# Two attention layers on one core: projections in half blocks, and four split steps in the second layer

## The chip, the core and the metric

The kernel runs on one core of a Trainium2 chip. The core has five engines with queues of their own, which wait for each other through semaphores: PE (TensorE, matrix products; its weight loads are shown as PEld), DVE (VectorE, elementwise work), ACT (ScalarE, exponentials and copies), POOL (GpSimd) and SP (SyncE, which here only issues DMAs). The metric is the device time of one execution, in microseconds (us).

## What is computed

Two self-attention layers over four images of 64 x 64 pixels (4096 tokens) with 256 channels, in float32. Cut to what matters:

```python
# layer 0: queries and keys have 32 channels, values 256
q, k, v = x @ Wq + bq, x @ Wk + bk, x @ Wv + bv
x = gamma * softmax(q @ k.T) @ v + x
# layer 1: queries and keys have 32 channels, values 128, then back to 256
f, g, v = x @ Wf + bf, x @ Wg + bg, x @ Wh + bh
x = x + (softmax(g @ f.T) @ v) @ Wo + bo
```

The softmax runs over all 4096 tokens of an image, and the result is x after both layers.

## The kernel before

**Stages.** Image after image, first layer, then second layer. The code calls the layers `l = 0` and `l = 1`. A block of queries is 256 tokens in the first layer (16 blocks) and 512 in the second (8 blocks). Each block runs over all keys in steps: 8 steps of 512 keys in the first layer, 16 steps of 256 keys in the second. So every step has 128 x 1024 scores, and there are 128 steps per layer and image, 1024 in all. The list `steps` (line 645) holds them, and the loop of line 654 walks it.

**A step.** `Step.scores` (line 498) multiplies keys by queries into the PSUM tile `st`, of which there is only one, and ACT takes the exponential into `p`. The scores of step s are issued two steps ahead (`later`, line 685). [...] So some steps are *split*: ACT writes a second exponential `high`, a little smaller than `p` (line 515); DVE forms `low = p - high` (line 522, one step ahead) and `d` from low and high (line 527); the values are cut in the same way into h, l and d; and three F32R products (high, low, d) take the place of one plain product (`products_first`, line 531, `products_second`, line 544). In the first layer all steps are split. In the second those with `i % 5 == 2`: steps 2, 7 and 12 of each block (line 248). In the second layer DVE also adds every `p` to `p_sum` (line 698), since the softmax's divisor comes from there; line 696 opens it with a copy at each block's first step.

**Projections.** `project_units` (line 405) makes queries, keys and values of one block of 512 tokens, as a list of units: a transpose unit (line 371: DVE turns 32 x 32 squares that eight DMAs of `load_squares`, line 267, have laid out; ACT and DVE cut the result into two parts xh and xl), a qk unit (line 408: four matmuls of 512 columns into `psqk`, four small operations on ACT and DVE, a store to `qk_dram`, from which POOL's queue later loads `k` and `q`), and one or two value units (line 437). The queries, keys and values of the second layer are projected while the first layer still runs over later blocks, and those of the next image's first layer during the second layer. Values of the second layer live in the tags `v1` (plain) and `v1_parts` (split). For image 0, `AHEAD = 3` blocks are projected before the first step and the others in the steps of the first block (`early`, line 689), through PE transposes of `x_nat`.

**Ends.** `end_first` (line 566) normalises a block of the first layer, adds the residual and stores the result as x1_dram (for the projection) and x1_res (for the second residual). `end_second` (line 607) gives four output units, each two matmul groups (`pso`), a reciprocal, a multiply-add and a store.

**Order.** Units wait in a list `units`: the end units of the block before, then projections. Lines 702 to 705 release them at an even pace per step. The engines' queues may depart a little from the order in the program, for instance where the profile shows six products between two scores.[...]

Of the kernel before, what the change touches and what calls it, by code (L numbers as in the profile page):

```python
# [55 lines left out]
P = 128  # L57
QB = 512
# [4 lines left out]
EPS = 2.0**-12  # L63
AHEAD = 3

# [168 lines left out]
def fast_path(ctx: ExitStack, tc: tile.TileContext, x, w0, w1, wo, bo, gamma, out, off):  # L234
# [13 lines left out]
    split = [[l == 0 or i % 5 == 2 for i in range(NI[l])] for l in range(2)]  # L248
# [18 lines left out]
    def load_squares(key, tokens):  # L267

        turned[key] = []
        for c in range(NCC):  # L270
            t = work.tile([P, QB], F32, tag="squares", bufs=5, name=f"squares_{key[0]}_{key[1]}_{key[2]}_{c}")
            for a in range(P // S):
                ch = c * P + a * S
                nc.sync.dma_start(
                    t[a * S : (a + 1) * S, :].rearrange("j (b i) -> j b i", i=S),
                    tokens[:, ch : ch + S].rearrange("(b j) i -> j b i", j=S),
                )
            turned[key].append(t)

    def load_block(b, j):  # L280
        if b < B and j < NB:
            load_squares((b, 0, j), x[b, j * QB : (j + 1) * QB, :])


    x_nat = {}

    def load_first(j):
        if j < NB:
            x_nat[j] = []
            for n in range(j * NT, (j + 1) * NT):  # L290
                x_nat[j].append(data.tile([P, C], F32, tag="v1", bufs=V1, name=f"x_nat_{n}"))
                nc.sync.dma_start(x_nat[j][-1], x[0, n * P : (n + 1) * P, :])

    load_first(0)
    load_first(1)
# [8 lines left out]
    seen_v = const.tile([P, 2, B * NB, 2], F32, name="seen_v")  # L304
# [61 lines left out]
    xT, x_parts, k_t, v_t = {}, {}, {}, {}  # L366
# [4 lines left out]
    def transpose_unit(b, l, j):  # L371
        def issue():
            xT[b, l, j] = data.tile([P, NCC, QB], F32, tag="xT", name=f"xT_{b}_{l}_{j}")
            for c in range(NCC):
                if b == l == 0:
                    ps = side_psum(f"psx_{j}_{c}")
                    for t in range(NT):
                        nc.tensor.transpose(ps[:, t * P : (t + 1) * P], x_nat[j][t][:, c * P : (c + 1) * P], ident)
                    nc.scalar.copy(xT[b, l, j][:, c, :], ps)
                else:  # L380
                    nc.vector.transpose(xT[b, l, j][:, c, :], turned[b, l, j][c])
            x_parts[b, l, j] = []
            for c in range(NCC):
                parts = [
                    work.tile([P, QB], F32R, tag="squares", bufs=5, name=f"x{what}_{b}_{l}_{j}_{c}") for what in "hl"
                ]
                nc.scalar.copy(parts[0], xT[b, l, j][:, c, :])  # L387
                nc.vector.tensor_sub(parts[1], xT[b, l, j][:, c, :], parts[0].bitcast(F32))  # L388
                x_parts[b, l, j].append(parts)
            if b == l == 0:  # L390
                load_first(j + 2)
            elif l == 0:
                load_block(b, j + 1)
            elif j == NB - 1:
                load_block(b + 1, 0)

        return issue

    def split_values(v, h, low, d, seen):
        nc.scalar.activation(h, v, AF.Copy, scale=1.0 - DOWN)  # L400
        nc.scalar.activation(low, v, AF.Abs, accum_out=seen)
        nc.vector.scalar_tensor_tensor(d, h.bitcast(F32), -1.0 - EPS, v, ALU.mult, ALU.add)
        nc.vector.scalar_tensor_tensor(low, d.bitcast(F32), 1.0 / EPS, h.bitcast(F32), ALU.mult, ALU.add)

    def project_units(b, l, j):
        key = (b, l, j)

        def qk_unit():
            ps = side_psum(f"psqk_{b}_{l}_{j}")
            for c in range(NCC):  # L410
                for n in range(2):
                    nc.tensor.matmul(  # L412
                        ps,
                        wqk[l][:, c, :],
                        x_parts[key][c][n],
                        start=(c == n == 0),
                        stop=(c == NCC - 1 and n == 1),
                    )
            whole = data.tile([2 * D, QB], F32, tag="qk", name=f"qk_{b}_{l}_{j}")
            parts = data.tile([P, QB], F32R, tag="qk_parts", name=f"qk_parts_{b}_{l}_{j}")  # L420
# [6 lines left out]
            qk_dram[key] = dram.tile([2, 2, D, QB], F32, name=f"qk_dram_{b}_{l}_{j}")  # L427
            nc.sync.dma_start(qk_dram[key].rearrange("h w d n -> (h w d) n"), parts.bitcast(F32))
            if b == l == 0:
                near = parts.rearrange("(h w d) n -> h w d n", h=2, w=2)  # L430
                load_k(b, l, j, near)
                if j == 0:
                    load_q(b, l, j, near)

        per = QB // CV[l]

        def v_unit(t0):
            def issue():
                ps = side_psum(f"psv_{b}_{l}_{j}_{t0}").rearrange("p (t c) -> p t c", c=CV[l])
                for t in range(per):  # L440
                    for c in range(NCC):
                        nc.tensor.matmul(  # L442
                            ps[:, t, :],
                            xT[key][:, c, (t0 + t) * P : (t0 + t + 1) * P],
                            wv[l][:, c, :],
                            start=(c == 0),
                            stop=(c == NCC - 1),
                        )
                tiles = slice(t0, t0 + per)
                seen = [seen_v[:, l, b * NB + j, n : n + 1] for n in range(2)]  # L450
                if l == 0:
                    split_values(ps, *(v0[j][what][:, tiles, :C] for what in ("h", "l", "d")), seen[t0 // per])
                    return
                for n in range(NT // G[1]):
                    i = j * NT // G[1] + n
                    v = ps[:, n * G[1] : (n + 1) * G[1], :]
                    if split[1][i]:
                        t = data.tile([P, 3, G[1], P], F32R, tag="v1_parts", bufs=sum(split[1]), name=f"v_{b}_{i}")
                        v_t[b, i] = {what: t[:, m] for m, what in enumerate(("h", "l", "d"))}
                        split_values(v, *v_t[b, i].values(), seen[n])  # L460
                    else:
                        v_t[b, i] = data.tile([P, G[1], P], F32, tag="v1", bufs=V1, name=f"v_{b}_{i}")
                        nc.scalar.copy(v_t[b, i], v)
                        nc.scalar.activation(v, v, AF.Abs, accum_out=seen[n])  # L464

            return issue

        return [transpose_unit(b, l, j), qk_unit] + [v_unit(t0) for t0 in range(0, NT, per)]

    def load_rows(dst, parts, which, halves):  # L470
        for n, h in enumerate(halves):
            nc.gpsimd.dma_start(dst[n * D : (n + 1) * D, :], parts[h, which])  # L472

    def load_q(b, l, j, parts=None):
        q_t[b, l, j] = data.tile([P, QB], F32R, tag="q", bufs=2, name=f"q_{b}_{l}_{j}")
        load_rows(q_t[b, l, j], qk_dram[b, l, j].bitcast(F32R) if parts is None else parts, 0, (0, 0, 1, 1))

    def load_k(b, l, j, parts=None):
        k_t[b, l, j] = data.tile([P, QB], F32R, tag="k", bufs=NB, name=f"k_{b}_{l}_{j}")
        load_rows(k_t[b, l, j], qk_dram[b, l, j].bitcast(F32R) if parts is None else parts, 1, (0, 1, 0, 1))  # L480
# [8 lines left out]
    class Step:  # L489
# [28 lines left out]

# [5 lines left out]
        def cut_both(self):  # L524
            if self.split:
                self.d = wide("d" if self.l == 0 else "l", f"d_{self.key}", F32R)
                nc.vector.scalar_tensor_tensor(  # L527
                    self.d, self.low.bitcast(F32), -1.0 / EPS, self.high.bitcast(F32), ALU.mult, ALU.add
                )

# [13 lines left out]
        def products_second(self, acc):  # L544
            v = v_t[self.b, self.i]
            some = [i for i in range(NI[1]) if split[1][i]]
            for p, v, which, first, last in (
                (
                    (self.high, v["h"], 0, self.i == some[0], False),
                    (self.low, v["l"], 0, False, self.i == some[-1]),  # L550
                    (self.d, v["d"], 1, self.first, self.last),
                )
                if self.split
                else ((self.p, v, 1, self.first, self.last),)
            ):
                for g in range(G[1]):
                    nc.tensor.matmul(  # L557
                        acc[which],
                        v[:, g, :],
# [6 lines left out]
    def end_first(b, j, acc):  # L566
# [11 lines left out]
        def residual(s):  # L578
            def issue():
# [11 lines left out]
                if part == QB // QB0 - 1 and s == NS - 1:  # L591
                    load_squares((b, 1, jj), x1_dram[b, jj])
# [49 lines left out]
    for j in range(AHEAD):  # L642
        run(project_units(0, 0, j))
# [7 lines left out]
    units, done, acc, p_sum = bias_units(), 0, None, None  # L651
    keys = [(b, l, j) for b in range(B) for l in range(2) for j in range(NB)][NB:]

    for n, s in enumerate(steps):
        b, l, j = s.b, s.l, s.j
        if s.first:
            done = 0
# [139 lines left out]
```

## Time and profile before

Three runs took 3223.26, 3223.30 and 3223.58 us. The profiled execution is one further run.

| | |
|---|---|
| median of 3 runs | 3223.3 us |
| profiled execution, its own time | 3222.18 us |
| its span, first to last instruction | 3220.4 us |
| granted TensorE clock, mean | 0.998 |
| DMA, mean over the span | 53 GB/s |
| queue of SP, share of 16 engines | 16.0% |
| queue of POOL, share of 16 engines | 4.5% |

The starts of the second layer's blocks can be read from line 696, the copy that opens p_sum. The distances between them, in us:

| image | block 0 to 1 | 1 to 2 | 2 to 3 | 3 to 4 | 4 to 5 | 5 to 6 | 6 to 7 |
|---|---|---|---|---|---|---|---|
| 0 | 48.56 | 39.50 | 41.75 | 41.77 | 41.72 | 41.75 | 41.76 |
| 1 | 50.19 | 39.49 | 41.75 | 41.77 | 41.73 | 41.76 | 41.77 |
| 2 | 50.20 | 39.50 | 41.77 | 41.75 | 41.76 | 41.76 | 41.74 |
| 3 | 41.25 | 35.88 | 37.16 | 37.18 | 37.16 | 37.52 | 36.81 |

In images 0 to 2 the next image is projected beside these blocks; in image 3 there is none. In the first layer two blocks together, one with a projection and one without, take 56.5 us. The first block of the first image ends at 95 us.

The profile names an instruction by line, engine and operation, output and inputs, and the shape (partitions x elements). "x4" is a number of instructions that follow each other; a bracket at a line's end says how long the engine was idle before it and what ended the wait.

### The profile page before, as it was taken

Reading aid. Unit: us, or ns where it says so; the run is one execution under the profiler, and the core shown is the slowest. Engines: PE = TensorE matmul, PEld = TensorE weight load, DVE = VectorE, ACT = ScalarE, POOL = GpSimd, SP = SyncE. Lnnn points to the kernel's source line nnn. Section 1 sums busy time; section 2 is a strip of 40 time slices with the busy share of each in tenths; the row PEclk is TensorE's granted clock in tenths of the full one; section 3 lists DMA queues with packets and bytes.
Section 4 is the critical chain, followed back from the end, with each engine's and each line's share of the span. In section 5 each row is a group of like instructions: output and inputs, shape, how many; then the busy total and the mean of one; then the engine's idle time right before and its main releaser. Section 6 shows DMA issues by size and latency. Waiting matters only on the chain. (4 is left out here: it accounts for less than half of the span.)

```text
span 3220.4 us, 51144 instructions
## 1 busy us (share of the span) xinstructions
PE 3166.5 (98%) x19460; PEld 2613.0 (81%) x19460; DVE 2691.5 (84%) x3181; ACT 1988.8 (62%) x2483; POOL 661.3 (21%) x784
## 2 busy tenths in 40 slices
PE   8999999999999999999999999999999999999998
PEld 7999997566799999655679999966558999995554
DVE  7888888888888888788888888878888888887776
ACT  6666666655566666565556666655555666665554
POOL 3222223000232222200022222310002222241000
PEclk9999999999999999999999999999999999999999
DMA  4111123221212112322121112232222211121110
GB/s 120 47 47 44 50 50 83 56 53 49 59 44 54 44 52 49 79 53 53 49 64 42 49 50 50 61 70 52 51 52 57 53 41 47 46 70 47 36 36 31
DMA packets 368653, 172.16 MB, mean 53 GB/s; under 512 B 257392, under 2 KB 343664, under 8 KB 368400
## 3 DMA queue, kind: packets, MB, share of 16 engines
q1 hardware_dynamic: 342528, 134.29, 16.0%
q0 software_dynamic: 24960, 34.18, 4.5%
q8 instruction: 157, 2.57, 0.3%
q14 instruction: 96, 0.79, 0.1%
q10 hardware_dynamic: 912, 0.33, 0.0%
HBM read 99.22 MB, written 67.11 MB: 52 GB/s over the span
## 5 line engine op out<-in xcount | busy, mean ns | idle before, releaser
L517 ACT ACTIVATE p<-st 128x1024 f32<-128x1024 f32 x1024 | 1044.5, 1020 | 393.6 <-PE st L505 369.5
L515 ACT ACTIVATE high<-st,down 128x1024 fp32r<-128x1024 f32 x608 | 678.8, 1116 | 683.6 <-PE st L505 572.7
L527 DVE SCALAR_TENSOR_TENSOR d<-low,high 128x1024 fp32r<-128x1024 f32 x608 | 761.2, 1252 | 208.3 <-PE acc L536 202.9
L522 DVE TENSOR_TENSOR low<-p,high 128x1024 fp32r<-128x1024 f32 x608 | 810.6, 1333 | 134.2 <-ACT p L517 134.2
L557 PE MATMUL acc<-p,v 128*128 128x512 f32 x1664 | 795.2, 597 | 0.0
L505 PE MATMUL st<-q,k 128*128 128x256 f32 (+1 forms) x3072 | 778.6, 361 | 8.4 <-ACT p L517 8.3
L698 DVE TENSOR_TENSOR p_sum<-p_sum,p 128x1024 f32<-128x1024 f32 x480 | 587.1, 1223 | 60.7 <-ACT p L517 47.5
L505 PEld LDWEIGHTS st<-q,k 128*128 128x128 f32 x3072 | 461.2, 189 | 210.7 <-ACT p L517 113.3
L536 PE MATMUL acc<-v0d,d 128*128 128x258 f32 x4096 | 591.7, 284 | 1.7 <-DVE d L527 1.6
L536 PE MATMUL acc<-v0h,high 128*128 128x258 f32 x4096 | 588.6, 283 | 1.6 <-ACT high L515 1.6
L536 PE MATMUL acc<-v0l,low 128*128 128x258 f32 x4096 | 587.0, 283 | 0.5 <-DVE low L522 0.5
L536 PEld LDWEIGHTS acc<-v0d,d 128*128 128x128 f32 x4096 | 533.1, 189 | 6.7 <-DVE d L527 3.6
L536 PEld LDWEIGHTS acc<-v0h,high 128*128 128x128 f32 x4096 | 534.1, 190 | 3.4 <-ACT high L515 2.0
L536 PEld LDWEIGHTS acc<-v0l,low 128*128 128x128 f32 x4096 | 532.7, 189 | 0.8 <-DVE low L522 0.7
L557 PEld LDWEIGHTS acc<-p,v 128*128 128x128 f32 x1664 | 308.4, 190 | 214.3 <-issue 184.7
L593 POOL TENSOR_TENSOR x_res<-x,bo 128x256 f32<-128x256 f32 x128 | 216.3, 1690 | 889.9 <-DVE g L583 482.0
L472 POOL DMA_DIRECT2D q<-qk_dram x252 | 123.9, 501 | 1166.1 <-PE st L505 1143.0
L676 POOL TENSOR_TENSOR x_res<-x_res,bv 128x256 f32<-128x256 f32 x128 | 189.6, 1482 | 114.4 <-DMA x_res<-in_x 85.0
L442 PE MATMUL psv<-wv,xT 128*128 128x128 f32 (+1 forms) x1024 | 194.8, 331 | 6.8 <-DVE qk L423 6.1
L442 PEld LDWEIGHTS psv<-wv,xT 128*128 128x128 f32 x1024 | 159.6, 192 | 29.8 <-DVE qk L423 8.5
L472 POOL DMA_DIRECT2D k<-qk_dram x224 | 109.6, 500 | 245.2 <-PE st L505 140.3
L388 DVE TENSOR_TENSOR xl<-xT,xh 128x512 fp32r<-128x512 f32 x128 | 87.1, 683 | 5.1 <-ACT xh L387 4.7
(96 smaller groups left out, 1701.9 us busy)
## 6 DMA issues: line engine op xcount, KB each, us to landing
x_res<-in_x SPq DMA_DIRECT2D x128, 128.0 KB, 2.2
qk_dram<-qk_parts SPq DMA_DIRECT2D x64, 256.0 KB, 2.1
x_dram<-x SPq DMA_DIRECT2D x128, 128.0 KB, 1.7
x_res<-x_res SPq DMA_DIRECT2D x128, 128.0 KB, 1.7
squares<-x_dram SPq DMA_DIRECT2D x256, 64.0 KB, 2.3
x_old<-x_res SPq DMA_DIRECT2D x128, 128.0 KB, 2.0
out<-x_old SPq DMA_DIRECT2D x128, 128.0 KB, 1.7
q<-qk_dram POOLq DMA_DIRECT2D x252, 64.0 KB, 2.1
```

The lines of the kernel that those rows point to most:

```text
L442: nc.tensor.matmul(ps[:, t, :], xT[key][:, c, (t0 + t) * P : (t0 + t + 1) * P], wv[l][:, c, :], start=(c == 0), stop=(c == NCC - 1),)
L472: nc.gpsimd.dma_start(dst[n * D : (n + 1) * D, :], parts[h, which])
L505: nc.tensor.matmul(st[:, g, :], k_t[b, l, kt // NT][:, kt % NT * P : (kt % NT + 1) * P], q_t[b, l, j * n // QB][:, q0 : q0 + n], start=Tru ...
L515: nc.scalar.activation(self.high, s_flat, AF.Exp, bias=down)
L517: nc.scalar.activation(self.p, s_flat, AF.Exp)
L522: nc.vector.tensor_sub(self.low, self.p, self.high.bitcast(F32))
L527: nc.vector.scalar_tensor_tensor(self.d, self.low.bitcast(F32), -1.0 / EPS, self.high.bitcast(F32), ALU.mult, ALU.add)
L536: nc.tensor.matmul(acc[2 * s + which][:, :W], p[:, g * QB0 + s * P : g * QB0 + (s + 1) * P], v0[self.i][v][:, g, :], start=self.first and ...
L557: nc.tensor.matmul(acc[which], v[:, g, :], p[:, g * QB : (g + 1) * QB], start=first and g == 0, stop=last and g == G[1] - 1,)
L593: nc.gpsimd.tensor_add(x_old[s], x_new[s], bo_sb)
L676: nc.gpsimd.tensor_add(x_res[b, j][t], x_res[b, j][t], bv)
L698: nc.vector.tensor_add(p_sum, p_sum, s.p)
```

## The change

Projections are cut into halves of 256 tokens (`h`, 16 per image and layer; `QB0 = 256`, `NH = N // QB0`). A half has one transpose unit over both halves of the channels, one qk unit with four matmuls of 256 columns, and one value unit. Squares, xT, xh and xl have one buffer each. In image 0's first layer xT, xh, xl and the parts of qk use the four buffers of `v1_parts` instead. The list with a pace is replaced by `plan`, which gives each unit a step. In the second layer steps 2, 6, 10 and 14 are split instead of 2, 7 and 12.

```diff
+UP = 2.0**12
+SPLIT1 = (2, 6, 10, 14)
...
-    split = [[l == 0 or i % 5 == 2 for i in range(NI[l])] for l in range(2)]
+    NH = N // QB0
+    split = [[l == 0 or i in SPLIT1 for i in range(NI[l])] for l in range(2)]
...
     def load_squares(key, tokens):
+        t = work.tile([P, NCC, QB0], F32, tag="squares", bufs=1, name="squares_" + "_".join(map(str, key)))
         for c in range(NCC):
-            t = work.tile([P, QB], F32, tag="squares", bufs=5, name=f"squares_{key[0]}_{key[1]}_{key[2]}_{c}")
...
-    load_first(0)
-    load_first(1)
+    for h in range(LEAD):
+        load_first(h)
...
-    def transpose_unit(b, l, j):
+    def transpose_unit(b, l, h):
         def issue():
+            key = (b, l, h)
+            lead = b == l == 0
+            tag = "v1_parts" if lead else "xT"
+            xT[key] = data.tile([P, NCC, QB0], F32, tag=tag, bufs=LEAD_BUFS if lead else 1, name=f"xT_{b}_{l}_{h}")
             if b == l == 0:
+                ps = side_psum(f"psx_{h}").rearrange("p (c n) -> p c n", c=NCC)
+                for c in range(NCC):
+                    for t in range(NS):
+                        nc.tensor.transpose(ps[:, c, t * P : (t + 1) * P], x_nat[h][t][:, c * P : (c + 1) * P], ident)
+                nc.scalar.copy(xT[key], ps)
+            else:
+                nc.vector.transpose(
+                    xT[key].rearrange("p c n -> p (c n)"), turned[key].rearrange("p c n -> p (c n)")
+                )
...
+            nc.scalar.copy(x_parts[key][0], xT[key])
+            nc.vector.tensor_sub(x_parts[key][1], xT[key], x_parts[key][0].bitcast(F32))
+            if b == l == 0:
+                load_first(h + LEAD)
             elif l == 0:
-                load_block(b, j + 1)
-            elif j == NB - 1:
-                load_block(b + 1, 0)
+                load_half(b, h + 1)
+            elif h == NH - 1:
+                load_half(b + 1, 0)
...
         def qk_unit():
-            ps = side_psum(f"psqk_{b}_{l}_{j}")
+            ps = side_psum(f"psqk_{b}_{l}_{h}")[:, :QB0]
...
+            nc.sync.dma_start(qk_dram[b, l, j].rearrange("h w d n -> (h w d) n")[:, cols], parts.bitcast(F32))
+            halves[b, l, j] = part + 1
             if b == l == 0:
                 near = parts.rearrange("(h w d) n -> h w d n", h=2, w=2)
-                load_k(b, l, j, near)
+                load_k(b, l, j, cols, near)
...
-                if part == QB // QB0 - 1 and s == NS - 1:
-                    load_squares((b, 1, jj), x1_dram[b, jj])
+                if s == NS - 1:
+                    load_squares((b, 1, j), x1_dram[b, jj][part * QB0 : (part + 1) * QB0, :])
...
-    for j in range(AHEAD):
-        run(project_units(0, 0, j))
+    lead = [project_units(0, 0, h) for h in range(2 * AHEAD)]
+    run([u[0] for u in lead[:2]])
+    for h in range(2 * AHEAD):
+        run(lead[h][1:])
+        run([u[0] for u in lead[h + 2 : h + 3]])
...
+    def plan(b, l, j, ends):
+
+        units = {}
+
+        def put(i, *some):
+            units.setdefault(i, []).extend(some)
+
+        if l == 0:
+
+            if j >= 2:
+                t, qk, v = project_units(b, 1, j - 2)
+                put(0, t), put(4, qk), put(5, v)
+            for n, u in enumerate(ends):
+                put(1 + n, u)
+            return units
+        if j == 0:
+            for n, u in enumerate(ends):
+                put(1 + n, u)
+            for n, h in enumerate((NH - 2, NH - 1)):
+                t, qk, v = project_units(b, 1, h)
+                put(6 * n, t), put(6 * n + 2, qk), put(6 * n + 3, v)
+        else:
+            for n, u in enumerate(ends):
+                put(1 + n, u)
+        if b + 1 < B:
+            for h in range(NH):
+                i = 10 + 7 * h - j * NI[1]
+                for n, u in zip((0, 2, 3), project_units(b + 1, 0, h)):
+                    if 0 <= i + n < NI[1]:
+                        put(i + n, u)
+        return units
...
-        pace = NI[l] - (5 if l == 1 else 1)
-        upto = min(len(units), -(-len(units) * (s.i + 1) // pace))
-        todo = units[done:upto]
-        done = upto
+        s.add_up(p_sum)
+        todo = units.get(s.i, [])
...
-        while keys and keys[0] in qk_dram and (keys[0][:2] == (b, l) or keys[0][2] < over):
+        while keys and halves.get(keys[0]) == 2 and (keys[0][:2] == (b, l) or keys[0][2] < over):
```

## The prediction

> **What bounds the kernel now.** I read the page's busy shares first, then the windows of one stretch of each stage, then the timeline of single steps, then the waits of the one stage that runs unevenly.
>
> ```profile
> PE 3166.5 (98%) x19460; PEld 2613.0 (81%) x19460; DVE 2691.5 (84%) x3181; ACT 1988.8 (62%) x2483; POOL 661.3 (21%) x784
> ```
>
> PE is busy throughout, but a modelled busy PE need not run at its best, so each stage is checked against the pitch of its own matmuls. The windows (columns: PE, PEld, DVE, ACT, POOL busy, clock, DMA share) are one second-layer block with next image's projections beside it, one without (image 3), and two first-layer blocks with one projection:
>
> ```profile
> 2239.60:2281.35 41.75, 41.50 (x140) 24.97 (x139) 35.47 (x44) 24.63 (x31) 1.95 (x4) 1.00 0.21 51
> 3055.06:3092.22 37.16, 36.85 (x121) 21.22 (x119) 29.18 (x34) 19.95 (x21) 1.94 (x4) 1.00 0.12 35
> 2506.10:2562.60 56.50, 56.50 (x470) 56.34 (x469) 48.51 (x55) 37.28 (x47) 14.61 (x12) 1.00 0.18 47
> ```
>
> In the first layer weight loads are dense too (56.34 of 56.50): 448 matmuls at 0.12 us are 53.8, a projection 0.92 + 1.78, together 56.5. Nothing is lost there, and only fewer matmuls would help. In the second layer PE leaves small holes. The timeline of the last block gives the pitch of its two kinds of step:
>
> ```profile
> 3186.48 0.63 PE L557 MATMUL acc<-high,v 128*128 128x512 f32 x2
> 3186.94 0.62 PE L557 MATMUL acc<-low,v 128*128 128x512 f32 x2
> 3187.41 0.64 PE L557 MATMUL acc<-d,v 128*128 128x512 f32 x2
> 3187.88 0.62 PE L505 MATMUL st<-q,k 128*128 128x512 f32 x2
> ...
> 3190.31 1.02 PE L505 MATMUL st<-q,k 128*128 128x512 f32 x2
> 3191.17 1.88 PE L557 MATMUL acc<-p,v 128*128 128x512 f32 x4
> 3192.48 1.03 PE L505 MATMUL st<-q,k 128*128 128x512 f32 x2
> ```
>
> From start to start, two fp32r matmuls take 0.46 us; a whole step (two scores, four product matmuls) takes 2.17. A step in three products is 4 x 0.46 = 1.84, so it saves 0.33. An output unit takes 0.57 (pso to the next acc in the same view). A block of image 3 should be 13 x 2.17 + 3 x 1.84 + 4 x 0.57 = 36.0; it takes 37.2. The timeline of a split step with no unit beside it (step 12 of that block) shows where the rest goes:
>
> ```profile
> 3082.04 1.11 ACT L515 ACTIVATE high<-st,down 128x1024 fp32r<-128x1024 f32 x1 [1.16 <-PE st L505]
> ...
> 3084.10 1.23 DVE L522 TENSOR_TENSOR low<-p,high 128x1024 fp32r<-128x1024 f32 x1 [1.96 <-ACT p L517]
> ...
> 3085.24 1.22 DVE L698 TENSOR_TENSOR p_sum<-p_sum,p 128x1024 f32<-128x1024 f32 x1
> ...
> 3086.38 1.22 DVE L527 SCALAR_TENSOR_TENSOR d<-low,high 128x1024 fp32r<-128x1024 f32 x1
> ...
> 3087.65 0.30 PEld L557 LDWEIGHTS acc<-d,v 128*128 128x128 f32 x2 [0.73 <-DVE d L527]
> ```
>
> The reader is to see one chain: two exps, low, the running sum, d; PE has done everything else and stands 0.7 us for d. The other 0.45 us of the block falls on its other two splits, about 0.2 each; they have output units beside them. So a bare split costs about 0.7, and wins nothing: 0.33 - 0.7.
>
> Last, the waits of the first second-layer block of image 1, where units are crowded:
>
> ```profile
> PEld acc L557 <- DVE d L527: 2.5, 2, 2.0
> PEld psv L442 <- DVE qk L423: 2.3, 1, 2.3
> PE st L505 <- ACT p L517: 1.9, 2, 1.7
> ```
>
> By the starts of p_sum, the first two blocks of images 0, 1, 2 last 88.1, 89.7, 89.7 us, where two regular ones and one more projection (0.92 + 1.78) would be 86.2: 8.9 us lost in all. In image 3 nothing is lost (77.1 against 77.0).
>
> [...]
>
> **The change, part by part.** The sum is made against the profiled execution, 3222.2 us (span 3220.4 and 1.8 around it); the median of the runs, 3223.3, lies 1.1 above.
>
> *One more split step in each second-layer block* (2, 6, 10, 14 instead of 2, 7, 12; 32 steps in all). PE: -0.33 each. ACT: one more high, 1.1 us; ACT has 17 us free in the block and is no bound. DVE: low and d, 2.4 us. In image 3: steps 2 and 6 have outputs beside them (outputs now at steps 1 to 4), 0.2 each; 10 and 14 are bare, 0.7 each: loss 1.8 instead of 1.15, block 35.7 + 1.8 = 37.5, +0.3. Eight blocks: **+2.5**.
>
> *Images 0 to 2.* A regular block is 41.76; PE's own work is 36.0 + 4.40 (qk 4 x 0.23, values 16 x 0.2175, from the eight loads of psv that follow each other in 1.74) = 40.4; loss 1.35, of which 1.15 as in image 3 and 0.2 from crowding. After: -0.33, and qk in eight matmuls of 256 at 0.12 instead of four at 0.23, +0.04: 40.1. Values come at steps 13 + 7h of the stage; three in four of them fall into the three steps that end with a split, 12 of 28 splits, and their 1.74 us of PE cover the chain. So steps 10 and 14 lose 2 x 0.7 x 16/28 = 0.8, step 6 about 0.15, step 2 0.2: 1.15. That makes 41.25 plus crowding on DVE. DVE was busy 35.5 of 41.75. It gets 2.44 for the split; 0.37 for the halved bias and remainder (0.74 + 0.69 before, twice 0.48 + 0.42 after, from the 256-column rows); and 1.0 since a half every 7 steps is 16/7, not 2, halves per block: 39.3 of 41.3. The trace shows no block so full. Bounds of crowding: 0 (the units no longer come in lumps) to 1.6 (each split's d waits for one 512-column op, 0.6 start to start, in two to three of four). I take 0.5: even pieces help, a nearly full queue hurts. Block 41.75, no gain: **0.0** over 24 blocks.
>
> *The first block of the stage.* Half 14 comes at steps 0, 2, 3, half 15 at 6, 8, 9, next image's first at 10, 12, 13: the jam is spread. Half 15 still has a chain: residual at step 2, its store (1.7 us to landing), eight square loads behind it on SP (0.47 us issue each, 2.3 to landing), transpose, qk, store 2.1, four k loads on POOL at 0.5, landing 2.1. It arrives about step 12, when scores of step 14 need it. I leave 1.5 us lost in each image instead of 1.9, 3.5, 3.5, 0.1: **-3.0**. Bounds: -9 to +4.
>
> *The first layer.* Transpose, two residuals, qk, values now in every block instead of every second. DVE's 48.5 of 56.5 gains 0.4; each step leaves about 0.9 us between low and the next d, which waits for PE's d products anyway, and one 512-column op fits. SP issues 16 square loads instead of 8 per pair of blocks, +4 us in 56; POOL's queue is unchanged except for the start. Only the extra qk time shows: 40 blocks here and at the start x 0.04: **+1.6**. If the cover fails, 0.5 us in each of 56 blocks, 28 us; I hold that unlikely, since every second block already shows it without a hole.
>
> *The start* (95 us to the end of the first block; PE's work 69 of it). Smaller pieces start earlier, six halves are loaded ahead; against that four buffers carry xT, xh, xl and parts, and POOL issues twice as many k loads from parts (+16 us of its time). **0**, bounds -5 to +7. *The end*: step 14 split instead of 12 just before the last products: **+0.4**.
>
> Sum: 2.5 + 0.0 - 3.0 + 1.6 + 0.4 = +1.5, **3224 us**.
>
> **Rivals.**
> Faster: the even spread is worth what it looks like. Crowding 0.1 instead of 0.5 (-9.6), the jam gone entirely (-5.9), the start 3 us shorter: 3205. For it: DVE's work fits, ACT is 60% busy, and the first layer shows that PE can be kept dense at 86% DVE. Against: the bare splits, which spreading does not touch in image 3.
> Slower: DVE becomes late at the splits of images 0 to 2. Place: the transposes and xl, or the value ops, queued between low and d, with PE's d products behind them. Price: two of four splits 0.6 us late, crowding 1.4 instead of 0.5, 24 x 0.9 = 22: 3246. It costs time from 0.44 of crowding a block up, and more than 0.2% from about 0.7. For it: 39.3 of 41.3. Against: d is issued ahead of the same step's units.
> A change that does not do what it says: "evenly" holds only while there is a next image; image 3 keeps four splits and no units. That is in the sum.
>
> **How the numbers follow.** Forecast (3216 to 3232) 0.42, faster case 0.25, slower case 0.33. What this kernel's measurement can tell from no change is 0.2%, 6.4 us. Of the forecast's own spread about 0.05 lies below and 0.2 above that bound. Faster 0.27, same 0.32, slower 0.41. The range takes in both rivals' centres: 3203 to 3251.
>
> **What would show it.** Image 3: p_sum starts 37.5 apart, and d waits of 0.7 at steps 10 and 14. Images 0 to 2: starts 41.3 + crowding apart; below 41.4 the faster case, above 42.5 the slower, then with PEld waits for DVE d and low several times the present 30 us. First-layer pairs of blocks stay at 56.5; if they grow, the cover argument is wrong. End of the first block off 95 by more than 7: the start was misjudged.

## The result, and the profile after

Seven runs of the changed kernel took 3229.1 to 3235.4 us, median 3233.6; seven of the kernel before beside them 3222.7 to 3224.3, median 3223.6. The ratio is 1.003 (95% interval 1.0018 to 1.0042): slower by 0.3%, some 10 us. The profiled execution took 3233.45, its span 3231.7.

The sum of busy times, as before the change:

```profile
PE 3174.0 (98%) x19780; PEld 2643.9 (82%) x19780; DVE 2783.9 (86%) x3381; ACT 2034.5 (63%) x2643; POOL 672.0 (21%) x820
```

DVE has 200 instructions and 92 us more, ACT 46 us more, PE 7 us more. Part of it is the qk unit, whose operations on half the columns take more than half the time: the two on DVE 472 and 432 ns at 64x256 (L442, L444) against 740 and 694 at 64x512 (L423, L425 before), the two on ACT 370 and 402 against 584 and 620. That is 24 of DVE's 92 us and 22 of ACT's 46. None of this says where 11 us of span went. For that the span is cut at four kinds of marks: the end of the first first-layer block (the start of its addition of `o`), the copy that opens p_sum in each image, the first such addition of the next image, and the last copy. Each row adds over its images:

| part, us | before | after | difference | predicted |
|---|---|---|---|---|
| start, to the end of the first block | 95.3 | 111.2 | +15.9 | 0 |
| first layer, from there to the first copy, four images | 1696.3 | 1697.7 | +1.3 | +1.6 |
| second layer of images 0 to 2, to the end of the next image's first block | 1112.0 | 1095.5 | -16.5 | -4.4 |
| second layer of image 3, first to last copy | 263.0 | 269.9 | +7.0 | +4.3 with the next row |
| last copy to the end | 53.9 | 57.5 | +3.6 | |
| span | 3220.4 | 3231.7 | +11.3 | +1.5 |

So little in the total hides two large changes of opposite sign. The windows (PE, PEld, DVE, ACT, POOL busy, clock, DMA share, GB/s) of ten us of the start, before and after the change, then of the changed kernel's two blocks of image 2, a regular block of image 3 and two first-layer blocks:

```profile
10.00:20.00 10.00, 8.55 (x32) 5.85 (x30) 6.80 (x12) 5.73 (x12) 5.29 (x10) 1.00 0.75 221
10.00:20.00 10.00, 6.43 (x22) 5.00 (x21) 4.12 (x10) 3.81 (x9) 5.38 (x10) 0.74 0.68 208
2241.38:2285.68 44.30, 44.30 (x157) 27.99 (x156) 40.23 (x53) 28.25 (x41) 1.95 (x4) 1.00 0.23 55
2285.68:2326.08 40.40, 40.37 (x143) 25.09 (x142) 37.16 (x47) 25.50 (x34) 1.95 (x4) 1.00 0.24 55
3022.64:3060.54 37.90, 37.18 (x122) 21.45 (x121) 31.10 (x35) 20.98 (x23) 1.94 (x4) 1.00 0.12 35
2507.26:2563.75 56.49, 56.49 (x475) 56.49 (x474) 49.10 (x56) 37.50 (x49) 15.55 (x12) 1.00 0.19 48
```

The reader sees four things. In the start no engine is busy for more than two thirds of that stretch, where PE was busy for 86% before. The blocks beside a next image are no longer of one length: the two shown, with 22 and 16 instructions of value products (`psv`), take 44.3 and 40.4 us. Image 3's regular block takes 37.9 us instead of 37.2. A pair of first-layer blocks is as long as before.

The timeline of a bare split, step 10 of a block of image 3:

```profile
2969.16 1.02 ACT L538 ACTIVATE p<-st 128x1024 f32<-128x1024 f32 x1
...
2970.21 1.23 DVE L542 TENSOR_TENSOR low<-p,high 128x1024 fp32r<-128x1024 f32 x1 [1.82 <-ACT p L538]
2970.23 0.44 PEld L526 LDWEIGHTS st<-q,k 128*128 128x128 f32 x2 [0.42 <-ACT p L538]
...
2971.36 1.22 DVE L557 TENSOR_TENSOR p_sum<-p_sum,p 128x1024 f32<-128x1024 f32 x1
...
2972.49 1.22 DVE L547 SCALAR_TENSOR_TENSOR d<-low,high 128x1024 fp32r<-128x1024 f32 x1
...
2973.76 0.30 PEld L582 LDWEIGHTS acc<-d,v 128*128 128x128 f32 x2 [0.77 <-DVE d L547]
```

As before, d stands behind the running sum of its own step, and PE waits 0.77 us for d. These waits have moved from one image to another. For the second layer of image 2 (columns: us in total, times, longest), before and after:

```profile
PEld acc L557 <- DVE d L527: 7.3, 9, 2.0
PEld acc L582 <- DVE d L547: 4.3, 9, 0.8
```

and for that of image 3, to the end of the run:

```profile
PEld acc L557 <- DVE d L527: 7.7, 10, 2.0
PEld acc L582 <- DVE d L547: 12.9, 16, 1.3
```

Over images 0 to 2 they fell from 21.9 to 13.2 us.

### The profile page after: what moved, and what is told of

The parts are those of the page before. It is cut to its first block, busy times and chain, and to the rows that moved or that the text cites. A ratio compares the mean times of both kernels' runs of the same rounds, so it can differ in the third digit from the quotient of the medians.

```text
span 3231.7 us, 53309 instructions
## 1 busy us (share of the span) xinstructions
PE 3174.0 (98%) x19780; PEld 2643.9 (82%) x19780; DVE 2783.9 (86%) x3381; ACT 2034.5 (63%) x2643; POOL 672.0 (21%) x820
## 5 line engine op out<-in xcount | busy, mean ns | idle before, releaser
L536 ACT ACTIVATE high<-st,down 128x1024 fp32r<-128x1024 f32 x640 | 714.7, 1117 | 704.9 <-PE st L526 576.2
L547 DVE SCALAR_TENSOR_TENSOR d<-low,high 128x1024 fp32r<-128x1024 f32 x640 | 812.3, 1269 | 188.2 <-PE acc L564 178.3
L542 DVE TENSOR_TENSOR low<-p,high 128x1024 fp32r<-128x1024 f32 x640 | 839.5, 1312 | 116.2 <-ACT p L538 115.6
L526 PE MATMUL st<-q,k 128*128 128x256 f32 (+1 forms) x3072 | 762.0, 355 | 8.1 <-ACT p L538 5.4
L582 PE MATMUL acc<-p,v 128*128 128x512 f32 x1536 | 730.6, 596 | 0.0
L582 PEld LDWEIGHTS acc<-p,v 128*128 128x128 f32 x1536 | 282.4, 190 | 202.4 <-issue 177.9
L618 POOL TENSOR_TENSOR x_res<-x,bo 128x256 f32<-128x256 f32 x128 | 205.2, 1604 | 851.7 <-DVE x L610 851.6
L489 POOL DMA_DIRECT2D k<-qk_dram x224 | 111.3, 506 | 220.7 <-PE st L526 126.4
L582 PE MATMUL acc<-high,v 128*128 128x512 f32 x256 | 101.7, 478 | 2.3 <-ACT high L536 2.3
```

The source lines that it names most:

```text
L526: nc.tensor.matmul(st[:, g, :], k_t[b, l, kt // NT][:, kt % NT * P : (kt % NT + 1) * P], q_t[b, l, j * n // QB][:, q0 : q0 + n], start=Tru ...
L536: nc.scalar.activation(self.high, s_flat, AF.Exp, bias=down)
L542: nc.vector.tensor_sub(self.low, self.p, self.high.bitcast(F32))
L547: nc.vector.scalar_tensor_tensor(self.d, self.low.bitcast(F32), -UP, self.high.bitcast(F32), ALU.mult, ALU.add)
L582: nc.tensor.matmul(acc[which], v_part[:, g, :], p[:, g * QB : (g + 1) * QB], start=first and g == 0, stop=last and g == G[1] - 1,)
L618: nc.gpsimd.tensor_add(x_old[s], x_new[s], bo_sb)
```

## The experiments

All compare with the changed kernel unless an edit says otherwise. Each was timed beside the kernel before, whose median was 3223.4 to 3224.1 each time; intervals are those of the ratio to it.

**Two sets of buffers at the start.** The waits up to 112 us of the changed kernel show who waits for the single ring of four `v1_parts` buffers:

```profile
ACT xT L388 <- PE psqk L424: 8.6, 4, 3.0
...
DVE xl L404 <- PE psv L460: 6.0, 3, 3.0
...
PE psqk L424 <- DVE v0d L478: 5.1, 3, 3.1
```

ACT's copy into xT doesn't read psqk, nor does xl read psv. They wait until those products have read the buffer that they are to fill. The third line is a wait for a side bank of PSUM.

```diff
-            lead = b == l == 0
+            lead = b == l == 0 and h % 2 == 1
```

(in both places; even halves then use the tags xT, xh, xl and qk_parts)

> Image 0's projections take two sets of buffers in turn: even halves the tags xT, xh, xl and qk_parts, which stand empty then, odd halves the four buffers of v1_parts. If the shared ring of four is what made the start 15.9 us longer (111.2 instead of 95.3 us to the end of the first block), that end falls to 96 to 100 us and the whole to about 3220 (3218 to 3223). Rival, the size of the pieces itself (48 tiles through two side banks of PSUM instead of 40, longer chains per token, twice as many k loads on POOL): the first block still ends after 107 us and the whole stays at 3230 to 3234. All that follows the first block is the same either way.

Measured: 3219.8 us, ratio 0.9988 (0.998 to 0.9997). The first block ends at 101.0. None of these three is left in the same view of this run. Among the longest on these tiles there are

```profile
ACT qk L441 <- PE psqk L424: 8.9, 9, 1.9
...
PEld psqk L424 <- ACT xT L388: 4.5, 5, 1.7
```

The first is a wait for data. The second isn't: psqk doesn't read xT, and the copy into xT is what empties a side bank. So the shared ring made 10.2 of the 15.9 us, give or take one: in the runs below that leave the start of the changed kernel alone its first block ends between 109.8 and 111.3, in those with two sets between 100.3 and 101.0. The end at 101 lies just outside the first theory's 96 to 100, and the other 5.7 us stay open: smaller pieces, the two side banks and POOL's k loads were not told apart.

The time fell by 13.8, more than the start. Of the rest, 2.2 us lie in the second block of image 3, 38.1 instead of 40.4, which this edit doesn't touch; the last section speaks of it. That the time fell on the expected 3220 is in part luck.

**d ahead of the running sum.** The edit asks for another order in DVE's queue and nothing else.

```diff
-                nc.vector.tensor_add(p_sum, p_sum, self.p)
+            elif self.split:
+                with tc.issue_after(self.d_ins.ins):
+                    nc.vector.tensor_add(p_sum, p_sum, self.p)
```

> In the second layer's split steps, d is put ahead of the running sum of the same step on DVE, so it starts 1.2 us earlier. If d behind p_sum is what makes a bare split cost time, the waits of 0.77 us for d at steps 10 and 14 of image 3 go, its blocks fall from 37.9 to about 37.0, and the whole by 7 to 14 us, to 3220 to 3227. Rival, the single score tile st with two exponentials is the limit (PE's weight load waits 0.42 for exp p at each bare split): PE then waits there instead, blocks stay above 37.6, the whole above 3230.

Measured: 3216.1 us, 0.9976 (0.9967 to 0.9985), 17.5 less than the changed kernel. Image 3's regular blocks take 37.04. The timeline of the same step:

```profile
3033.12 1.23 DVE L542 TENSOR_TENSOR low<-p,high 128x1024 fp32r<-128x1024 f32 x1 [1.50 <-ACT p L538]
3033.14 0.44 PEld L526 LDWEIGHTS st<-q,k 128*128 128x128 f32 x2 [0.42 <-ACT p L538]
...
3034.46 1.23 DVE L547 SCALAR_TENSOR_TENSOR d<-low,high 128x1024 fp32r<-128x1024 f32 x1
...
3035.60 1.22 DVE L558 TENSOR_TENSOR p_sum<-p_sum,p 128x1024 f32<-128x1024 f32 x1
...
3035.92 0.41 PEld L585 LDWEIGHTS acc<-d,v 128*128 128x128 f32 x2
```

d comes 1.3 us after low instead of 2.3, and at this step PE has no wait for it; at step 14 one of 0.30 is left, after one of 0.36 for low. The wait of 0.42 for exp p, ahead of the next scores, is unchanged, and such waits for exp p grow from 3.7 to 4.8 us in a block: the rival's limit exists, but comes second. The part of images 0 to 2 became 6.7 us shorter, image 3 7.4, the end 2.0. Some 2 of image 3's 7.4 are again its second block, where the changed kernel's clock was 0.72 in the first 5 us.

**The same order in the kernel before.** The same edit on the kernel before the change.

> The kernel before the change, with d ahead of the running sum of the same step in the second layer's split steps and nothing else. If the order on DVE cost time in the same way before, image 3's regular blocks fall from 37.2 to 36.6 to 36.8, and the whole by 6 to 14 us, to 3209 to 3217. If only the changed kernel, with its fuller DVE, suffers from it: 3220 to 3224.

Measured: 3207.0 us, 0.9948 (0.9934 to 0.9961), 17.1 less. Image 3's regular blocks 36.68, those of images 0 to 2 41.31 instead of 41.75. The loss was there before, and as a whole it is as large in both kernels. But it lies elsewhere: the order of d takes 14.3 us from images 0 to 2 of the kernel before and 1.5 from image 3, and 6.7 and 7.4 from those of the changed one. With d first in both kernels the change would look like this, from the two profiled executions:

| part, us | before, d first | after, d first | difference | difference as measured above |
|---|---|---|---|---|
| start | 96.6 | 111.3 | +14.7 | +15.9 |
| first layer | 1696.4 | 1697.3 | +0.9 | +1.3 |
| second layer of images 0 to 2 | 1097.7 | 1088.8 | -8.9 | -16.5 |
| second layer of image 3 | 261.5 | 262.6 | +1.1 | +7.0 |
| last copy to the end | 52.7 | 55.4 | +2.7 | +3.6 |

So half blocks and four splits gain 8.9 us in images 0 to 2 without d's lateness. The other 7.6 came from less of it, as units stand beside more of the splits. In the second layer of image 2 PE's weight loads wait more than 0.5 us for d at nine of 24 splits before and at five of 32 after; at none of the fourteen did a value or output product run in the 5 us ahead. Of image 3's 7.0 us 5.9 are not there with d first in both: the same lateness, with no units to cover it, and some 2 us of its second block, in whose first 5 us the changed kernel's clock was 0.72.

**Three splits.**

```diff
-SPLIT1 = (2, 6, 10, 14)
+SPLIT1 = (2, 7, 12)
```

(`v1_parts` keeps four buffers, `v1` gets a thirteenth)

> Half blocks and their plan stay, but the splits are at 2, 7 and 12 again. If the fourth split is neutral beside projections and a loss without them, image 3's regular blocks fall from 37.9 to 37.2 and the end by about 3, the blocks of images 0 to 2 move by less than 0.2 each, and the whole is 3220 to 3228. Rival, the fourth split earns its 0.33 us of PE where a next image is projected: images 0 to 2 get 0.3 a block longer, 8 us, and the whole is 3230 to 3236. Second rival, it costs there by crowding DVE: they get 0.5 shorter, and the whole is below 3216.

Measured: 3224.7 us, 1.0005 (0.9997 to 1.0013). Image 3's regular blocks took 38.0, not 37.2: none of the three expectations. Images 0 to 2 gained 4.0 together, the start 1.9, image 3 4.1, which lies in its first two blocks (75.8 instead of 80.4); the end lost 0.9. The start's 1.9 is hardly more than it varies by. The fourth split alone is not what lengthened image 3's regular blocks, but d's lateness still is. The waits for d in one regular block of image 3, in the kernel before and in this one:

```profile
PEld acc L557 <- DVE d L527: 0.7, 1, 0.7
PEld acc L582 <- DVE d L547: 1.5, 2, 0.7
```

Before, only step 12 of the three splits made PE wait; step 7 had an output unit near it. With the outputs at steps 1 to 4, steps 7 and 12 both stand bare. The block is 0.8 us longer, about one such wait.

**Outputs at their old steps.** What still differed in such a block of image 3 was the place of its output units. The kernel before had them at steps 0, 2, 5 and 8 there; in images 0 to 2 its pace put them at 0, 1, 2 and 4, so for those images the edit tries a new place.

```diff
-            for n, u in enumerate(ends):
-                put(1 + n, u)
+            for i, u in zip((0, 2, 5, 8), ends):
+                put(i, u)
```

(in blocks after the first)

> The four output units of a block come at steps 0, 2, 5 and 8, where the kernel before had them, instead of 1, 2, 3 and 4; all else is the changed kernel. If the outputs' place is what made image 3's blocks long (with three splits at the old steps they still took 38.0 us, against 37.2 before the change), regular blocks there fall from 37.9 to 37.0 to 37.3, and the whole by 6 to 16 us, to 3218 to 3228. Rival, the splits without cover are the cause whatever the outputs do: blocks stay at 37.7 to 38.0 and the whole above 3230.

Measured: 3227.4 us, 1.0014 (1.0007 to 1.002); image 3's regular blocks 37.73. That is the rival's figure for the block, while the time falls by 6.3; in the profiled execution 2.4 of that lies in the second block of image 3, 38.0 instead of 40.4, of which the last section speaks. With four splits the outputs' place alone is worth 0.17 a block, and a regular block still has two waits for d, 1.4 us in all. With three splits it is worth 0.8, if the kernel before (37.2, three splits, outputs at 0, 2, 5, 8) is set against the run with three splits: a reading across two kernels, not a run of its own. In the same way a fourth split costs 0.6 with the outputs at their old steps (37.7 against 37.2). So neither the split nor the outputs' place is the cause alone. What the four kernels share is the number of waits for d in the block: one in the kernel before, two in the other three.

**The last half of the second layer.** Two edits on the same chain. The first only moves half 15 forward, and half 14's products by one step:

```diff
-                put(6 * n, t), put(6 * n + 2, qk), put(6 * n + 3, v)
+                put(5 * n, t), put(5 * n + 1, qk), put(5 * n + 2, v)
```

> Half 15 of the second layer comes at steps 5, 6 and 7 instead of 6, 8 and 9, half 14 at 0, 1, 2. If the chain store, square loads, transpose, qk, store, k loads, scores of step 14 is what stops PE at the end of the first block of the stage (about 4 us in image 3), that block becomes 2 to 4 us shorter in image 3 and 1 to 2 in the others, and the whole 3 to 9 us shorter, 3225 to 3231. Rival, its squares are not there at step 5, since they are loaded behind the residual of step 2: DVE then waits with its transpose and the running sums behind it, and the block gets longer by up to 2 us; the whole 3234 to 3242.

Measured: 3234.4 us, 1.0035 (1.0023 to 1.0047), nothing gained; image 3's first block takes 39.8 instead of 40.0. The time is that of the rival, but the block is no longer. The timeline of the changed kernel shows what the chain waits for:

```profile
2903.59 0.48 DVE L610 SCALAR_TENSOR_TENSOR x<-o,g,x_res 128x256 f32<-128x256 f32 x1
...
2911.23 0.48 DVE L610 SCALAR_TENSOR_TENSOR x<-o,g,x_res 128x256 f32<-128x256 f32 x1
...
2915.22 3.87 SPq L278 DMA_DIRECT2D squares<-x_dram  x8
...
2931.20 1.99 POOL L489 DMA_DIRECT2D k<-qk_dram  x4 [17.39 <-DMA qk_dram<-qk_parts]
```

The second residual, planned for step 2, runs 7.6 us after the first, behind running sums; all else of the chain hangs on its store. Then both residuals were put at step 0 as well:

```diff
         if j == 0:
-            for n, u in enumerate(ends):
-                put(1 + n, u)
+            put(0, *ends)
```

> In the first block of the second-layer stage both residual units come at step 0 (they came at 1 and 2), half 14 at steps 0, 1, 2 and half 15 at 5, 6, 7. If the late second residual (7.6 us behind the first, with running sums between) is what delays half 15, its store comes some 4 us earlier, k is there before the scores of step 14, the first block falls from 40.0 to about 37.5 in image 3 and the second, whose clock was lowered after the stall, from 40.4 to about 38: the whole 3226 to 3230. Rival, the chain is as long with the residual early, since DVE takes the transpose and the small operations late: the block stays above 39.5 and the whole at 3232 to 3236.

Measured: 3217.0 us, 0.9981 (0.9973 to 0.9988), 16.6 less than the changed kernel, more than expected.

```profile
2892.32 0.48 DVE L610 SCALAR_TENSOR_TENSOR x<-o,g,x_res 128x256 f32<-128x256 f32 x1
...
2896.54 0.48 DVE L610 SCALAR_TENSOR_TENSOR x<-o,g,x_res 128x256 f32<-128x256 f32 x1
...
2916.07 1.98 POOL L489 DMA_DIRECT2D k<-qk_dram  x4 [16.93 <-DMA qk_dram<-qk_parts]
```

The second residual comes 4.2 us after the first. From the first residual to the k loads it is 23.8 us instead of 27.6. The run has both edits, so the gain belongs to the pair. Image 3's first block falls from 40.0 to 36.8 and the second from 40.4 to 37.9; images 0 to 2 gain 3.2 each. The start, which the edits don't touch, is 1.4 shorter in this execution.

**Together.** Two sets and d first:

> Two sets of buffers at the start, and d ahead of the running sum, together. If the two effects are in different stages they add up: 3233.6 - 13.8 - 17.5 = 3202, a little more since both took away the same slowed block of image 3 (about 2 us): 3201 to 3206. If they share more than that: above 3208.

Measured: 3205.0 us, 0.9943 (0.993 to 0.9957): they add up but for 2.7 us, within what was expected. With the outputs at 0, 2, 5 and 8 besides:

> Two sets of buffers, d ahead of the running sum, and the outputs at steps 0, 2, 5 and 8. If the outputs' place gives its gain beside the order of d as well: image 3's regular blocks 36.2 to 36.6 and the whole 3188 to 3198. If both remove the same wait: blocks about 37.0 and the whole 3200 to 3206.

Measured: 3195.2 us, 0.9914 (0.9901 to 0.9928). Image 3's regular blocks are 36.77, between the two expectations, the time as the first has it. With the residuals of the last run as the fourth edit:

> The four edits together: two sets of buffers at the start, d ahead of the running sum, outputs at steps 0, 2, 5 and 8, both residuals at step 0 with half 15 at steps 5, 6 and 7. If the residuals' gain (16.6 us against the changed kernel) is in the first blocks of the stage alone, it adds to the 3195.2 of the other three: 3178 to 3184. If the other edits have already taken part of it (the slowed block after the stall in image 3): 3184 to 3192.

Measured: 3187.4 us, 0.9884 (0.9869 to 0.9899). The residuals' gain shrank from 16.6 to 7.8: part of it overlaps with the other edits. Last, how many splits are worth having in this kernel, three at 2, 7 and 12, or five:

> The four edits, with splits at 2, 7 and 12. If the fourth split earns PE's 0.33 us per block once d isn't late, this is 32 x 0.33 = 10 us slower than the four edits with four splits. If the chain over the one score tile takes it all, it is within 3 us of them; if the fourth split costs DVE time beside projections, it is faster by more than 3.

> The four edits, with five splits, at 1, 4, 7, 10 and 13. If a split earns PE's 0.33 us, 10 us faster than with four. If the score chain (two exponentials, about 2.9 us against 1.84 of PE, three plain steps' slack of 0.26 each) or DVE (2.4 us more of each 41) is the bound by then, it is slower than with four, by 5 to 20 us.

Measured: 3184.7 us, 0.988 (0.9865 to 0.9895), with three and 3188.7, 0.989 (0.9875 to 0.9905), with five. Image 3's regular blocks take 36.68, 36.75 and 37.01 with three, four and five splits, the part of images 0 to 2 1075.5, 1076.9 and 1076.5. A further split saves PE 0.33 by the forecast's price (in the trace of the kernel before, four matmuls of a plain product 0.43 us apart against six of the three F32R products 0.23 apart) and gives all of it back. Where it goes wasn't tried alone. With three and four splits a regular block of image 3 has no wait for d or low, but those for exp p, 4.3 and 4.5 us, which speaks for the score chain (the 2.9 us of the expectation is an estimate; in the changed kernel the scores after those of a bare split start 3.20 us behind them, at steps 10 and 14, and the two exponentials 1.01 apart); with five, waits of 0.37 for low and 0.32 for d are back at the last split. The number of splits also sets how many buffers `v1` and, with five, `v1_parts` have, and the starts differ by 2 us for it or by chance (98.5, 100.6 and 98.3). Three splits in half blocks with the four edits has the lowest median, 39 us under the kernel before; its lead over four splits, 2.7 us, is within the intervals.

## Why the prediction was right or wrong

The forecast time, 3224, was 9.6 us low. The measured 3233.6 lies inside the range and 1.6 above the likeliest case's own 3216 to 3232. That it came so near is luck for the most part: the start was off by +16 us, images 0 to 2 by -12, image 3 and the end by +6, and these nearly cancel.

- **The start** (0, bounds -5 to +7): wrong, +15.9. The step named the cause, "four buffers carry xT, xh, xl and parts", and priced it at nothing. A half needs all four, so the next half's copies wait for the products of the one before. The run with two sets gives 10.2 us for it; the rest is open.
- **Images 0 to 2, regular blocks** (0.0) and **first blocks** (-0.4, -2.0 and -2.0, the share of these images in the -3.0): measured -16.5 together. The starts of blocks put 14.9 of it into the first two blocks of the three images; the five after them take 41.88 on average, as if the forecast of 41.75 with its crowding of 0.5 had been right. But the plan moves work: in image 2 these five blocks hold 93 instructions of value products instead of 80. The forecast counted the additional share of a half for DVE and left it out for PE, and so its signs (41.4 and 42.5) can't be read as they stand. At the forecast's prices the moved products and their qk are about 0.8 us of PE a block, an estimate, so a block with the old work would take some 41.1, a little under the 41.25 without crowding. The crowding, 12 us in 24 blocks, is then the term that was too large. That fits the waits for d, which fell from 21.9 to 13.2 us here instead of growing, and the run with d first in both kernels: 7.6 of the 16.5 us are lateness of d that the change removed here. How the other 8.9 divide between first and regular blocks no run shows. In the first blocks more than the forecast's 1.5 us each was still to be had: the residuals at step 0, with half 15 moved forward, took out 3.2 in each of these images.
- **One more split in image 3** (+0.3 a block, 37.5): measured 37.9, with the waits for d of 0.77 at steps 10 and 14 as forecast. The mechanism, d behind the running sum at a split without cover, was shown by the run that reverses the two (-0.86 a block). Of a loss of 37.9 - 35.7 = 2.2 instead of 1.8, the two waits make 1.6 where 1.4 was forecast, so 0.6 is left for the rest, which had been put at 0.4. The label is too narrow: three splits in the same plan took 38.0. What counts is how many splits stand bare, and the outputs at steps 1 to 4, which the step mentions in brackets, bare one as a fourth split does.
- **First blocks, image 3** (+1.4 in the sum): its first two blocks took 80.4 instead of 77.1. The chain of half 15 that the step spelled out was the right one. Its second residual came 7.6 us after the first, which the plan's step number doesn't show. Some 2 us of the 3.3 lie in the second block, which took 40.4 us with a clock of 0.72 in its first 5 us, and 38.1 with two sets at the start, where the clock around the stall stayed at 1.00; the forecast couldn't know that.
- **The end** (+0.4): measured +3.6, mis-sized. With d first in both kernels +2.7 is left, so the order on DVE is about 0.9 of it; the rest is open.
- **First layer** (+1.6): the sum is right, +1.3, its place isn't. Pairs of blocks stayed at 56.5, and the cover held. The excess is in images 1 and 2, whose last pair takes 57.5 instead of 56.6.
- **The slower rival** had the right sign with the wrong place: it put DVE's lateness at the splits of images 0 to 2, where the waits for d fell. **The faster rival** was right for images 0 to 2, and lost to the start and to image 3.

## What to carry to other kernels

Where units are cut smaller and put through shared buffers, count how many one piece holds at a time and ask which reader frees the one that the next piece needs first. Read an engine's queue in the order that the trace shows, not by the step at which the program issues: here one running sum in front of a late operand cost 17.1 us in the kernel before and 17.5 in the changed one, and a residual behind running sums, with the half that waits for it, 16.6 alone and 7.8 beside the other edits. What such a lateness costs depends on what else the waiting engine has to do at that step: moving units beside the splits took 7.6 us of it from three images, and in the fourth, with the outputs moved to steps 1 to 4, a block of three splits had two waits for d, 1.5 us in all, instead of one of 0.7. A change whose total is small can be two large ones, so cut the span at fixed marks before looking for its cause.

## What was not expected of the hardware

The granted clock fell around short stalls in one execution, to 0.59, and not in another. In image 3 of the changed kernel, around the stall at the end of the first block, behind the late k (windows; the clock stands ahead of the last two figures):

```profile
2934.00:2939.00 5.00, 3.57 (x11) 1.50 (x9) 0.27 (x2) 2.03 (x2) 0.00 (x0) 1.00 0.03 9
2939.00:2944.00 5.00, 3.36 (x8) 1.87 (x9) 4.97 (x5) 2.71 (x4) 1.95 (x4) 0.59 0.22 52
2944.00:2949.00 5.00, 5.00 (x12) 2.74 (x11) 2.92 (x5) 1.61 (x2) 0.00 (x0) 0.72 0.00 0
```

and of the kernel with two sets at the start, where this stage is the same:

```profile
2923.00:2928.00 5.00, 3.75 (x11) 1.56 (x9) 0.56 (x1) 1.77 (x2) 0.00 (x0) 1.00 0.09 22
2928.00:2933.00 5.00, 3.18 (x11) 1.70 (x11) 4.68 (x5) 2.95 (x5) 1.94 (x4) 1.00 0.25 52
```

PE stands still for 3.1 us of ten in both, in several pieces. In the first the clock falls to 0.59 and the next block takes 40.4 us; in the second it stays at 1.00 and the block takes 38.1. So a stall of 3 us was followed by a block 2.3 us longer in one execution than in the other. With the outputs at 0, 2, 5 and 8 the clock stayed at 1.00 at the same place, and the second block took 38.0; in the run that only moved half 15 it took 39.6, and the clock over that whole run was 0.995, as in the changed kernel. In the first trace the waits of PE that make up the stall are 0.2 to 1.3 us each. What sets off the fall is not shown. In the start the clock was 0.74 and 0.75 from 10 to 30 us in the changed kernel, and 1.00 and 0.83 in the run with d first, whose first block ended at 111.3 all the same, against 111.2: the clock isn't what lengthened the start.
